# A graph layer on one core: one gather for the spare rows of two edge sets, and two sets given to the gathered path

## The chip, the cores and the metric

The kernel runs on one core of one Trainium2 chip. The metric is the device time of one execution in microseconds (us), taken as the median of several runs. TensorE is called PE in the profile (PEld is its weight loads), VectorE DVE, ScalarE ACT, GpSimd POOL; SP only issues DMAs here.

## The reference, cut to what matters

12,500 nodes with 128 features each, 400,000 edges, sorted by their destination. Each edge takes its source's row through one of two linear maps (by the edge's type), the results are summed by destination, a third map of the node itself is added, and relu, a residual and a layer norm follow:

```python
Xs = X[src]
m_data = Xs @ W_data.T + b_data
m_ctrl = Xs @ W_control.T + b_control
msg = jnp.where((edge_types == 0)[:, None], m_data, m_ctrl)
agg = jax.ops.segment_sum(msg, dst, num_segments=X.shape[0])
out = agg + (X @ W_self.T + b_self)
return jax.nn.relu(out)
...
x = _layernorm(x + _L0_gnn_ref(x, edge_index, edge_type_2, ...), axis=-1)
```

The kernel sums the raw source rows by destination and type first, and applies the maps to the sums.

## The kernel before, in words

**Rows.** Every row of x is split into three bf16 parts (384 values). They lie in SBUF as `x3`, in 98 blocks of 128 rows, and in device memory as `rows3`.

**Groups, chunks and sets.** The edges are 3125 chunks of 128. A group is 125 chunks, so there are 25 groups; each has five windows of 5 "p" chunks and 20 "e" chunks. `sets(g)` says how many of a group's five runs of 20 are handled as a *set*. In every fourth group it is all five, in the others four, and there the last window's 20 chunks go the way of the p chunks (25 in that window). This gives 107 sets and 985 gathered chunks. The main loop (L1066) has one turn, called a loop here, for each set `w`; `pairs` is the number of sets. Each loop takes its share of the gathered chunks, from the third loop on.

**The gathered path.** For a chunk, POOL issues one indirect DMA (`fetch`, L749 to L757) that brings 128 rows of 768 bytes from `rows3` into a tile `msg` (18 buffers), asked for 14 chunks ahead. `paced` (L759) ties each gather to a matmul on PE, so that it can't start before it; there are eleven such places in a loop, and a spare gather takes one of them before a chunk may. Later PE multiplies the rows by a 0/1 matrix of destinations, three matmuls and one for the counts (`gathered`, L772).

**The set path.** A set is 2560 edges. They are sorted into 100 cells, 98 of which stand for a block of 128 source rows, with 32 slots each. The cells lie as four quarters a (32 partitions each) by 25 columns q; column 24 holds blocks 96 and 97 and two empty quarters, 64 partitions. Two loops ahead of its use, the chain of set W runs (`give_slots`, L546): DVE builds the 0/1 matrix O of cells, PE counts the edges that stand ahead of each one (`before`, L579), DVE finds the ranks and the rank matrix, PE puts source row and destination code in their slots (`put`, L642), the slots are written to device memory and read back to all partitions (`spread`), DVE makes the pick matrix of them (L690), and the codes are turned and kept (`turn_codes` and `keep_codes`). In the set's own loop PE picks the rows out of `x3` by 98 matmuls (`pick`, L818), ACT copies them from PSUM (`rows`, L826), DVE makes the 0/1 matrix of destinations (`choose`) and PE adds (`add`, L847). This goes in five turns t = 0 to 4 (`unit`, L854); the end of a set (`end`, L883), with the last six columns, the chain's `tiled[5]` and the addition to the accumulator, is emitted within turn 0 of the next loop.

**Spare rows.** Edges with a rank of 32 or more find no slot. Up to 64 of them per set go to the spare half of column 24, and their rows come by a gather of 64 rows into the tile `last` (`spare_rows`, L796), issued in turn 1 of the set's loop and used by the last matmuls of the set. Its indices are made by `spare_slots` (L512) in four steps: a matmul that counts the spare edges of the partitions ahead (`over_before`, needs `over_n` of L619), a 0/1 matrix on DVE (`over_matrix`, tile `om_all`), seven matmuls (`turn`, needs `bits_b` of L629) and three copies on ACT (`keep`: the destination code, `part`, the index `idx`). For set w these steps ride in the chain of set w + 1: count and matrix after that chain's `before`, the last two in its `keep_codes`.

**PSUM.** All small products go through one bank, the tile `side` (one buffer): a chain's `ahead`, then its `rk`, the transposes of the finished groups and others take it in turn.

**Order.** Within an engine the instructions stand in an order that is planned when the program is built: mostly that of the code, but an instruction which the plan expects to wait may be passed by later ones. At run time each engine keeps its order. After every fourth or fifth loop a finished group is multiplied by the weights, normed and written (`finish`, L902), which makes those loops longer.

Of the kernel before, what the change touches and what calls it, by code (L numbers as in the profile page):

```python
# [17 lines left out]
P = 128  # L18
D = 128
# [10 lines left out]
NE = 5  # L30
# [10 lines left out]
CAP = 32  # L41
NBLK = -(-N // P)
NQ = 25
NCELL = 4 * NQ
OVF = 64
TOP = 7
# [104 lines left out]
def short_path(ctx, tc, const, ident, eps, wT, brow, bad, x, src, dst, etype, ws, bs, out):  # L151
# [23 lines left out]

    def sets(g):

        return NE if g % 4 == 0 else NE - 1

    def of_p(g, i):  # L180

# [111 lines left out]
    def iota(shape, pattern, base, mult, name):  # L293
        t = tmp.tile([P] + shape, I32, name=name)
        nc.gpsimd.iota(t, pattern=pattern, base=base, channel_multiplier=mult)
        return t
# [4 lines left out]
        nc.vector.tensor_copy(t, iota([n], [[1, n]], base, 0, f"{name}_i"))  # L301
        return t

    cell_col = keep.tile([P, NCELL], BF, name="cell_col")
    nc.vector.tensor_copy(cell_col.rearrange("p (a q) -> p a q", q=NQ), iota([4, NQ], [[1, 4], [4, NQ]], 0, 0, "i0"))
    for a, b in ((0, -1.0), (1, -1.0), (2, 96.0), (3, 97.0)):
        nc.vector.memset(cell_col[:, a * NQ + NQ - 1:a * NQ + NQ], b)
# [24 lines left out]
    slot_col = keep.tile([P, TOP, OVF], BF, name="slot_col")  # L332
    nc.vector.tensor_copy(slot_col, iota([TOP, OVF], [[-1, TOP], [1, OVF]], 0, 0, "i5"))

    om_all = keep.tile([P, TOP + 1, OVF], BF, name="om_all")
    nc.vector.memset(om_all, 0.0)

    ltri = keep.tile([P, 4, P], BF, name="ltri")
    free, own = iota([4, P], [[P // 4, 4], [1, P]], 0, 0, "i6"), iota([4], [[P // 4, 4]], 0, 1, "i7")
# [169 lines left out]
        )  # L509
        return sel  # L510

    def spare_slots(w, at):  # L512


        if w < 0:
            return [lambda: None] * 4
        s = slots[w]

        def over_before():
            nc.tensor.matmul(  # L520
                at["ahead"][:, 500:501], ltri[:, 0, :], over_n[:, w:w + 1], start=True, stop=True, skip_group_check=True
            )

        def over_matrix():
            s["om"] = om_all.rearrange("p k o -> p (k o)")
            nc.vector.tensor_scalar(om_all[:, :TOP], slot_col, at["ahead"][:, 500:501], None, op0=OP.is_equal)

        def turn():
            for k in range(TOP):
                nc.tensor.matmul(  # L530
                    at["rk"][:, 504:507], s["om"][:, k * OVF:k * OVF + P], s["bits"][:, :, k],
                    start=(k == 0), stop=(k == TOP - 1), skip_group_check=True,
                )

        def keep():
            code = s["code"][:OVF, NQ - 1:NQ]
            nc.scalar.copy(code, at["rk"][:OVF, 506:507].rearrange("p (n o) -> p n o", o=1).to_broadcast(list(code.shape)))
            part = two.tile([OVF, 2], FP, name="part")
            nc.scalar.copy(part, at["rk"][:OVF, 504:506])
            idx = two.tile([OVF, 1], I32, name="idx")  # L540
            nc.scalar.activation(idx, part[:, 0:1], AF.Identity, bias=part[:, 1:2], scale=128.0)
            s["idx"] = idx

        return [over_before, over_matrix, turn, keep]

    def give_slots(w):  # L546
# [32 lines left out]
        def before():  # L579
            s["ahead"] = side()  # L580
            cols = s["ahead"][:, :CQ * NCELL].rearrange("p (c j) -> p c j", j=NCELL)
            for a in range(4):
                cells = slice(a * NQ, (a + 1) * NQ)
                nc.tensor.matmul(  # L584
                    cols[:, :, cells], ltri[:, a, :], s["prod"][:, 2 * CQ:3 * CQ, cells],
                    start=(a == 0), stop=(a == 3), skip_group_check=True,
                )
            spares = s["spares"] = spare_slots(w - 1, s)
            spares[0]()

        def ranks():
# [80 lines left out]
        def keep_codes():  # L672
# [4 lines left out]
            nc.scalar.copy(code, at.to_broadcast(list(code.shape)))  # L677
# [116 lines left out]
        return evenly([lambda c=c: chunk(c) for c in range(n)])  # L794

    def spare_rows(w):  # L796
        msg = slots[w]["last"] = two.tile([P, 3 * D], BF, name="last")
        return nc.gpsimd.indirect_dma_start(  # L798
            out=msg[:OVF, :], out_offset=None, in_=rows3[:, :],
            in_offset=bass.IndirectOffsetOnAxis(ap=slots[w]["idx"], axis=0),  # L800
        )

    def picked(w, tiled, ending, before):

        g, i = each_e[w]
        s = {"sel": {}, "msg": {}}
        bounds = [0, 5, 10, 15, 19, NQ - 1]
        turns = len(bounds) - 1  # L810

        def choose(q0, n):

            sel = select(sp.tile([P, 10, 2 * EW], BF, name="esel")[:, :n], code_col, slots[w]["code"][:, q0:q0 + n])
            for k in range(n):
                s["sel"][q0 + k] = sel[:, k]

        def pick(ps, q, a0=0):  # L818
            for a in range(a0, 4):
                last = nc.tensor.matmul(  # L820
                    ps[CAP * a:CAP * (a + 1), :], slots[w]["pick"][:, a * NQ + q, :],
                    x3[:, 4 * q + a - a0].rearrange("p j d -> p (j d)"), start=True, stop=True, skip_group_check=True,
                )
            return last

        def rows(q, n, room, half=False):  # L826
            ps = psg.tile([P, room, 512], FP, name=f"got{room}")
            msg = two.tile([P, room, 3 * D], BF, name=f"emsg{room}")
            for k in range(n):
                last = pick(ps[:, k, :3 * D], q + k)  # L830
                s["msg"][q + k] = msg[:, k, :]
            if half:
                last = pick(ps[:, n, :3 * D], NQ - 1, 2)
            nc.scalar.copy(msg[:, :n], ps[:, :n, :3 * D])  # L834
            if half:
                nc.scalar.copy(s["msg"][NQ - 1][OVF:, :], ps[OVF:, n, :3 * D])
# [187 lines left out]

    def all_slots(w):
        units = begin_slots(w) + [u for _, u in begun.pop(w)]
        return units + [u for t in sorted(slots[w]["tiled"]) for u in slots[w]["tiled"][t]]

    split_units.pop(0)()
    prep_e(0)  # L1030
# [218 lines left out]
```

## Time and profile before

| | us |
|---|---|
| median of 3 runs (1748.27 to 1756.86) | 1756.15 |
| the profiled execution | 1757.87 |
| its span, first to last instruction | 1756.1 |

The profile is of one execution, whose granted TensorE clock was 0.995 of full speed on average. An engine's busy time is the time in which it executes; for PE the ends of matmuls are modelled. A row of a timeline has start, duration, engine, line, operation, the tiles written and read with their shapes, how many were merged into the row, and in brackets the engine's idle time before it with the instruction that ended it. A gather's duration on POOL is that of issuing it; the rows land later.

### The profile page before, as it was taken

To read this page: it belongs to the slowest core of one execution; us is meant where nothing else is said; L and a number is where in the kernel's file an instruction comes from. 1 tells how busy PE (TensorE), PEld (TensorE's weight loads), DVE (VectorE), ACT (ScalarE), POOL (GpSimd) and SP (SyncE) were. 2 spreads that over 40 slices of the span, in tenths; PEclk is the share of its full clock that TensorE was granted. 3 is DMA by queue.
4 is the path that set the end of the run, shared out by engine and by line. 5 is a ranking of instruction groups with operands and counts; after the bars stand their busy time and mean duration, and the time that the engine had idled before them with its cause. 6 is when DMAs were issued, how large, how long until landed. Compare 5 with 4: busy or idle time off the path is not lost.

```text
span 1756.1 us, 72083 instructions
## 1 busy us (share of the span) xinstructions
PE 1615.3 (92%) x29945; PEld 1311.7 (75%) x29945; DVE 1595.2 (91%) x3996; ACT 1229.2 (70%) x2249; POOL 1316.6 (75%) x1109
## 2 busy tenths in 40 slices
PE   0599999999999999999999999999999989999997
PEld 0377777777778777777877877777777777878786
DVE  8899999998999998999988999999999989999993
ACT  4577777767677667767766777776777766767675
POOL 0288877787777787877887877887877877777871
PEclk9999999999999999999999999999999999999999
DMA  8655454446454545444535454544454535544441
GB/s 237 209 165 160 128 158 136 147 125 199 115 164 134 159 125 179 143 152 127 166 119 164 150 164 133 164 122 147 160 159 135 158 108 162 167 139 141 151 139 41
DMA packets 190562, 261.28 MB, mean 149 GB/s; under 512 B 86437, under 2 KB 155983, under 8 KB 187152
## 3 DMA queue, kind: packets, MB, share of 16 engines
q1 hardware_dynamic: 126894, 148.02, 25.9%
q0 software_dynamic: 50704, 102.16, 20.8%
q10 hardware_dynamic: 12626, 6.40, 1.2%
q8 instruction: 236, 3.87, 0.9%
q14 instruction: 102, 0.84, 0.1%
HBM read 238.47 MB, written 18.00 MB: 146 GB/s over the span
## 4 chain that ended last, share of the span: by engine, by line
PE 48%; DVE 32%; issue 6%; DMA 6%; ACT 5%; DVEq 1%; POOL 1%; SPq 0%; POOLq 0%; ACTq 0%
PE sums L704 22%; PE got L820 15%; DVE esel L504 3%; PE side L950 3%; DVE pick L690 3%; PE sums L842 3%; DMA last<-rows,idx 3%; DVE rv L635 2%; ACT emsg L834 2%; DVE prod L598 2%; DVE prod L576 2%; PE side L584 2%; DVE acc L743 2%; PE side L647 2%; DVE ahead L594 2%
## 5 line engine op out<-in xcount | busy, mean ns | idle before, releaser
L754 POOL DMA_INDIRECT msg<-rows,pidx x985 | 1190.9, 1209 | 307.5 <-issue 118.9
L834 ACT CAST emsg<-got 128x768 bf16<-128x768 f32 (+1 forms) x1070 | 951.9, 930 | 303.9 <-PE got L820 289.8
L704 PE MATMUL sums<-esel,emsg 128*128 128x176 bf16 x7704 | 683.4, 240 | 0.0
L704 PEld LDWEIGHTS <-emsg 128*128 128x128 bf16 x7704 | 566.9, 98 | 68.7 <-issue 28.5
L820 PE MATMUL got<-x,pick 128*32 128x384 bf16 x10486 | 568.0, 330 | 21.9 <-DVE pick L690 14.7
L820 PEld LDWEIGHTS <-pick 128*32 128x32 bf16 x10486 | 239.2, 96 | 139.2 <-issue 20.6
L504 DVE TENSOR_TENSOR esel<-code_col,code 128x1760 bf16<-128x1760 bf16 x321 | 292.7, 912 | 13.6 <-PE sums L704 11.6
L798 POOL DMA_INDIRECT last<-rows,idx x107 | 122.0, 1141 | 106.0 <-DVE pick L690 63.7
L704 PE MATMUL sums<-psel,msg 128*128 128x48 bf16 x2955 | 184.2, 184 | 17.2 <-DVE acc L743 15.2
L842 PE MATMUL sums<-esel,one_col 128*32 128x176 bf16 x2675 | 193.7, 240 | 4.4 <-DVE acc L743 4.4
L704 PEld LDWEIGHTS <-msg 128*128 128x128 bf16 x2955 | 149.9, 97 | 36.2 <-issue 31.4
L842 PEld LDWEIGHTS <-one_col 128*32 128x32 bf16 x2675 | 111.9, 97 | 60.7 <-issue 4.1
L790 PE MATMUL sums<-psel,one_col 128*128 128x48 bf16 x985 | 150.2, 183 | 0.0
L743 DVE TENSOR_TENSOR acc<-acc,sums 128x352 f32 (+2 forms) x232 | 99.4, 430 | 40.4 <-PE sums L704 36.8
L504 DVE TENSOR_TENSOR O<-cell_col,blk 128x2000 bf16<-128x2000 bf16 x107 | 128.2, 1198 | 2.1 <-issue 2.1
L598 DVE TENSOR_TENSOR prod<-O,ahead 128x2000 bf16<-128x2000 bf16 x107 | 127.6, 1193 | 0.1
L690 DVE TENSOR_SCALAR pick<-pick,lane_f 128x3200 bf16<-128x3200 bf16 x107 | 113.2, 1058 | 0.0
L647 PE MATMUL side<-rv,O 128*128 128x64 bf16 x2140 | 83.3, 195 | 31.6 <-DVE rv L635 30.6
L647 PEld LDWEIGHTS <-O 128*128 128x128 bf16 x2140 | 78.7, 100 | 33.3 <-DVE rv L635 29.3
L594 DVE TENSOR_REDUCE ahead<-side 128x100 bf16<-128x500 f32 x107 | 72.2, 675 | 28.0 <-PE side L520 27.3
L790 PEld LDWEIGHTS <-one_col 128*128 128x128 bf16 x985 | 94.3, 96 | 0.0
L635 DVE TENSOR_TENSOR rv<-rm,vals 128x1280 bf16<-128x1280 bf16 x107 | 87.8, 821 | 0.3
(170 smaller groups left out, 1869.2 us busy)
## 6 DMA issues: line engine op xcount, KB each, us to landing
pick<-there SPq DMA_DIRECT2D x107, 800.0 KB
acc<-acc_start SPq DMA_DIRECT2D x23, 1280.0 KB
msg<-rows,pidx POOLq DMA_INDIRECT x985
rows<-x SPq DMA_DIRECT2D x6, 1344.0 KB
xs<-in_x_dram SPq DMA_DIRECT2D x99, 62.5 KB
out_dram<-h SPq DMA_DIRECT2D x99, 62.5 KB
xt<-in_x_dram ACTq DMA_DIRECT2D x6, 896.0 KB
there<-cell SPq DMA_DIRECT2D x107, 6.2 KB
```

The lines of the kernel that those rows point to most:

```text
L504: nc.vector.tensor_tensor(sel.rearrange("p n (w t) -> p n w t", t=2), col[:rows].rearrange("p (o w t) -> p o w t", o=1, t=2).to_broadcast( ...
L598: nc.vector.tensor_tensor(prod, s["O"], ahead.rearrange("p (o j) -> p o j", o=1).to_broadcast([P, EC, NCELL]), op=OP.mult)
L635: placed[:] = [nc.vector.tensor_tensor(rv.rearrange("p c v (r t) -> p c v r t", t=2), rm.rearrange("p c (o r t) -> p c o r t", o=1, t=2).t ...
L647: nc.tensor.matmul(s["rk"][:m, :2 * CAP], s["held"][:, c * NCELL:c * NCELL + m], s["rv"][:, c].rearrange("p v r -> p (v r)"), start=(c == ...
L690: nc.vector.tensor_scalar(t, t, lane_f, None, op0=OP.is_equal)
L704: last = nc.tensor.matmul(out, msg[:, j * D:(j + 1) * D], sel, start=(start and j == 0), stop=stop, skip_group_check=True)
L743: added.append(nc.vector.tensor_add(win, win, ps[:, :4 * wide].rearrange("p (a w) -> p a w", w=wide)[:, :, :width]))
L754: return nc.gpsimd.indirect_dma_start(out=msg, out_offset=None, in_=rows3[:, :], in_offset=bass.IndirectOffsetOnAxis(ap=codes["p", g][0][: ...
L790: nc.tensor.matmul(cnt, one_col, sel, start=False, stop=(c == n - 1), skip_group_check=True)
L820: last = nc.tensor.matmul(ps[CAP * a:CAP * (a + 1), :], slots[w]["pick"][:, a * NQ + q, :], x3[:, 4 * q + a - a0].rearrange("p j d -> p (j ...
L834: nc.scalar.copy(msg[:, :n], ps[:, :n, :3 * D])
L842: nc.tensor.matmul(cells_of(s["ps"], EW, 1)[CAP * (q % 4):CAP * (q % 4 + 1), :], one_col[:, :CAP], s["sel"][q], start=(q < 4), stop=(q + 4 ...
```

## The change

- `sets(g)` gives five sets in every sixth group instead of every fourth: 105 sets and 1025 gathered chunks.
- Even sets keep their layout: the spare rows in quarters 0 and 1 of column 24, blocks 96 and 97 in quarters 2 and 3. Odd sets are mirrored: blocks 96 and 97 lie in quarters 0 and 1, the spare rows in the other half. There are two tables of cells and two matrices `om_all`, one for each parity.
- One gather of 128 rows brings the spare rows of sets w and w + 1 (w even) into a tile `both` (one buffer). The odd set uses `both` directly. For the even set ACT copies the lower half into `last` (now one buffer) at the end of turn 4. The last set, 104, has no partner and is gathered alone, 64 rows.
- An odd set's spare slots are now made at the end of its own chain, so that both halves of the index are there for the even set's loop: `own_before` (count and matrix) goes with the code turns of the set's own chain and writes columns 508 and on of `rk`, `own_turn` (the seven matmuls and the three copies) comes at the end of turn 0 of the even set's loop. An even set's slots still ride in the next set's chain, which is odd; an even set's chain carries none.

```diff
     def sets(g):
-        return NE if g % 4 == 0 else NE - 1
+        return NE if g % 6 == 0 else NE - 1
...
-    om_all = keep.tile([P, TOP + 1, OVF], BF, name="om_all")
-    nc.vector.memset(om_all, 0.0)
+    om_all = [keep.tile([P, TOP + 1, OVF], BF, name=f"om_all{k}") for k in range(2)]
+    for t in om_all:
+        nc.vector.memset(t, 0.0)
...
-    def spare_slots(w, at):
+    def spare_slots(w, at, col=504):
...
-        def over_before():
+        def over_before(to="ahead", c=500):
+            s["before"] = at[to][:, c:c + 1]
             nc.tensor.matmul(
-                at["ahead"][:, 500:501], ltri[:, 0, :], over_n[:, w:w + 1], start=True, stop=True, skip_group_check=True
+                s["before"], ltri[:, 0, :], over_n[:, w:w + 1], start=True, stop=True, skip_group_check=True
             )
...
-            idx = two.tile([OVF, 1], I32, name="idx")
-            nc.scalar.activation(idx, part[:, 0:1], AF.Identity, bias=part[:, 1:2], scale=128.0)
-            s["idx"] = idx
+            part = two.tile([P, 2], FP, name="part")
+            nc.scalar.copy(part[half], at["rk"][half, col:col + 2])
+            if k == 0:
+                s["idx"] = two.tile([P, 1], I32, name="idx")
+            idx = slots[w - k]["idx"][half]
+            nc.scalar.activation(idx, part[half, 0:1], AF.Identity, bias=part[half, 1:2], scale=128.0)
...
-            select(s["O"], cell_col, blk2)
+            select(s["O"], cell_cols[w % 2], blk2)
...
-            spares = s["spares"] = spare_slots(w - 1, s)
+            spares = s["spares"] = spare_slots(w - 1 if w % 2 else -1, s)
...
+        def own_before():
+            s["own"] = spare_slots(w, s, 509)
+            s["own"][0]("rk", 508)
+            s["own"][1]()
+
+        def own_turn():
+            s["own"][2]()
+            s["own"][3]()
+
         s["tiled"] = {4: [put, spread], 5: [turn_codes, keep_codes]}
+        if w % 2:
+            s["tiled"][5] = [lambda: (turn_codes(), own_before()), keep_codes]
+            s["own_turn"] = own_turn
...
     def spare_rows(w):
-        msg = slots[w]["last"] = two.tile([P, 3 * D], BF, name="last")
+        n = P if w + 1 < pairs else OVF
+        both = two.tile([P, 3 * D], BF, name="both", bufs=1)
+        slots[w + 1 if n == P else w]["last"] = both
+        if n == P:
+            slots[w]["both"] = both
         return nc.gpsimd.indirect_dma_start(
-            out=msg[:OVF, :], out_offset=None, in_=rows3[:, :],
-            in_offset=bass.IndirectOffsetOnAxis(ap=slots[w]["idx"], axis=0),
+            out=both[:n, :], out_offset=None, in_=rows3[:, :],
+            in_offset=bass.IndirectOffsetOnAxis(ap=slots[w]["idx"][:n], axis=0),
         )
...
+        lead = 0 if w % 2 else 2
+        half_rows = slice(CAP * lead, CAP * lead + OVF)
...
             if half:
-                last = pick(ps[:, n, :3 * D], NQ - 1, 2)
+                last = pick(ps[:, n, :3 * D], NQ - 1, lead, lead + 2)
...
-                nc.scalar.copy(s["msg"][NQ - 1][OVF:, :], ps[OVF:, n, :3 * D])
+                nc.scalar.copy(s["msg"][NQ - 1][half_rows, :], ps[half_rows, n, :3 * D])
...
-            if t == 1 and w > 0:
+            if t == 1 and w > 0 and w % 2 == 0:
                 spare.append(lambda: spare_rows(w))
             if t == 3:
                 assert not spare
+                if "both" in slots[w]:
+                    slots[w]["last"] = two.tile([P, 3 * D], BF, name="last", bufs=1)
                 s["msg"][NQ - 1] = slots[w]["last"]
...
+            if t == 0 and w + 1 < pairs and "own_turn" in slots[w + 1] and w > 0:
+                slots[w + 1]["own_turn"]()
+            if t == turns - 1 and "both" in slots[w]:
+                nc.scalar.copy(slots[w]["last"][:OVF, :], slots[w]["both"][:OVF, :])
```

More of the change, by code (lines that the diff above doesn't have):

```diff
@@ L302, in table @@
         return t
[L304 to L307, printed above, removed]
+    cell_cols = [keep.tile([P, NCELL], BF, name=f"cell_col{k}") for k in range(2)]
+    cells_i = iota([4, NQ], [[1, 4], [4, NQ]], 0, 0, "i0")
+    for t, ends in zip(cell_cols, ((-1.0, -1.0, 96.0, 97.0), (96.0, 97.0, -1.0, -1.0))):
+        nc.vector.tensor_copy(t.rearrange("p (a q) -> p a q", q=NQ), cells_i)
+        for a, b in enumerate(ends):
+            nc.vector.memset(t[:, a * NQ + NQ - 1:a * NQ + NQ], b)
     rank_col = table(CAP, 0, "rank_col")
@@ L522, in over_before @@
             )
         def over_matrix():
-            s["om"] = om_all.rearrange("p k o -> p (k o)")
-            nc.vector.tensor_scalar(om_all[:, :TOP], slot_col, at["ahead"][:, 500:501], None, op0=OP.is_equal)
+            nc.vector.tensor_scalar(om[:, k:k + TOP], slot_col, s["before"], None, op0=OP.is_equal)
         def turn():
-            for k in range(TOP):
+            flat = om.rearrange("p k o -> p (k o)")
+            for j in range(TOP):
                 nc.tensor.matmul(
-                    at["rk"][:, 504:507], s["om"][:, k * OVF:k * OVF + P], s["bits"][:, :, k],
-                    start=(k == 0), stop=(k == TOP - 1), skip_group_check=True,
+                    at["rk"][:, col:col + 3], flat[:, j * OVF:j * OVF + P], s["bits"][:, :, j],
+                    start=(j == 0), stop=(j == TOP - 1), skip_group_check=True,
@@ L533, in turn @@
                 )
         def keep():
[L536 to L539, printed above, removed]
-            idx = two.tile([OVF, 1], I32, name="idx")
-            nc.scalar.activation(idx, part[:, 0:1], AF.Identity, bias=part[:, 1:2], scale=128.0)
-            s["idx"] = idx
+            code = s["code"][half, NQ - 1:NQ]
@@ new lines, in keep @@
+            nc.scalar.copy(
+                code, at["rk"][half, col + 2:col + 3].rearrange("p (n o) -> p n o", o=1).to_broadcast(list(code.shape))
+            )
+            part = two.tile([P, 2], FP, name="part")
[4 more added lines that the diff above has]
+            nc.scalar.activation(idx, part[half, 0:1], AF.Identity, bias=part[half, 1:2], scale=128.0)
@@ L816, in choose, with pick @@
                 s["sel"][q0 + k] = sel[:, k]
-        def pick(ps, q, a0=0):
-            for a in range(a0, 4):
+        lead = 0 if w % 2 else 2
+        half_rows = slice(CAP * lead, CAP * lead + OVF)
+        def pick(ps, q, a0=0, a1=4):
+            for a in range(a0, a1):
                 last = nc.tensor.matmul(
```

7 lines of the change are left out of this document (5 added, 2 removed).

## The prediction

> **What bounds the kernel now.** I read the page's first and fourth parts first, then the groups of instructions, the waits, and the stretches of the run. From the page:
>
> ```profile
> span 1756.1 us, 72083 instructions
> ...
> PE 1615.3 (92%) x29945; PEld 1311.7 (75%) x29945; DVE 1595.2 (91%) x3996; ACT 1229.2 (70%) x2249; POOL 1316.6 (75%) x1109
> ...
> PE 48%; DVE 32%; issue 6%; DMA 6%; ACT 5%; DVEq 1%; POOL 1%; SPq 0%; POOLq 0%; ACTq 0%
> ...
> L754 POOL DMA_INDIRECT msg<-rows,pidx x985 | 1190.9, 1209 | 307.5 <-issue 118.9
> ...
> L798 POOL DMA_INDIRECT last<-rows,idx x107 | 122.0, 1141 | 106.0 <-DVE pick L690 63.7
> ```
>
> By these shares POOL is idle for a quarter of the span, and the chain that ended last hardly touches it. The waits say otherwise (engine, line, releaser: us in total, times, longest):
>
> ```profile
> POOL msg L754 <- issue: 118.9, 390, 0.3
> POOL msg L754 <- PE got L820: 80.5, 249, 3.6
> POOL msg L754 <- PE sums L704: 51.9, 168, 1.0
> ...
> POOL last L798 <- ACT idx L541: 11.5, 5, 8.5
> ```
>
> 390 waits add up to 118.9 us and none is longer than 0.3: this is a fixed pause of 0.30 us after every gather, whoever is named as its releaser. The stretch in the middle shows what is left (PE, PEld, DVE, ACT and POOL busy):
>
> ```profile
> 82.00:1720.00 1638.00, 1570.09 (x29328) 1278.56 (x29325) 1515.15 (x3778) 1170.91 (x2166) 1301.01 (x1083) 1.00 0.48 147
> ```
>
> POOL works 1301.0 of 1638.0 us and pauses 1083 x 0.30 = 324.9, so only 12.1 us are free: **the gathers are a line without gaps**, 99% full. PE is 96% full, DVE 92%. PE does wait for POOL, at the spare rows, which have the shortest notice:
>
> ```profile
> PEld L704 <- DMA last<-rows,idx: 18.4, 14, 4.7
> PE sums L704 <- DMA last<-rows,idx: 15.2, 11, 4.5
> ```
>
> So POOL paces the kernel, and PE stands some 18 us behind it.
>
> **The change, part by part.**
>
> *Gathers.* Before, 985 chunk gathers and 107 spare gathers: 1092. After, 1025 chunk gathers and one spare gather for each pair, 53 (sets 0 and 1, ... , 102 and 103, then 104 alone): 1078, so 14 fewer. First and last start of either kind, with minimum, median and maximum ns:
>
> ```profile
> L754 POOL DMA_INDIRECT msg<-rows,pidx x985: 942/1043/4798, 73.2 to 1720.5; - x197
> ...
> L798 POOL DMA_INDIRECT last<-rows,idx x107: 911/1059/3007, 68.1 to 1729.9; - x107
> ```
>
> The start at 1720.5 is the 1091st (one spare gather follows): 1652.4 us over 1090 steps, 1.516 us each. 14 x 1.516 = **-21.2 us**. A pair's gather takes 128 rows where one took 64. The two kinds above are just these sizes: 942 ns against 911 at least, and the median of the larger is the smaller one. At most 52 x 0.031 = +1.6; I take **+1.6**, the lower end is 0.
>
> A gather is long where DVE works: one that starts beside a big DVE instruction takes 1.88 us, twice the minimum.
>
> ```profile
> 919.21 1.88 POOL L754 DMA_INDIRECT msg<-rows,pidx  x1 [0.30 <-DMA msg<-rows,pidx]
> ...
> 919.08 1.19 DVE L598 TENSOR_TENSOR prod<-O,ahead 128x2000 bf16<-128x2000 bf16 x1
> ```
>
> The time above the minima is 1190.9 + 122.0 - 985 x 0.942 - 107 x 0.911 = 287.5 us. Shared out over gathers it is in the 1.516. If it goes with the sets, whose DVE work the row shows beside a long gather, it is 2.69 us a set, and 14 x (0.942 + 0.30) + 2 x 2.69 = 22.8 us come off instead of 21.2. I keep 21.2 and 22.8 as the two ends. The Trainium skill ("SBUF — State Buffer", section "Who interferes with whom") says that a DVE instruction with two SBUF inputs contends with a GpSimd instruction that reads SBUF, which would make it the 22.8; the trace agrees as far as this row goes.
>
> *Two sets fewer, on PE.* A loop in which the chain of waits lies wholly on PE, between two ends of sets, and how closely chunks follow each other:
>
> ```profile
> 868.24 1.47 PE sums L704 x18
> ...
> 881.70 1.47 PE sums L704 x18
> ```
>
> ```profile
> 911.42 0.24 PE L704 MATMUL sums<-psel,msg 128*128 128x48 bf16 x3
> 911.50 0.18 PE L790 MATMUL sums<-psel,one_col 128*128 128x48 bf16 x1
> 911.53 0.23 PE L704 MATMUL sums<-psel,msg 128*128 128x48 bf16 x3
> ```
>
> 13.46 us a loop, 0.11 a chunk. With 985 / 105 = 9.4 chunks in it, a set alone costs 12.4: 2 x 12.4 - 40 x 0.11 = 20.5 us less on PE. Without the 18 us of stalls PE could end at 1756.1 - 18 - 20.5 = **1717.6**. PE therefore falls as much as POOL, and POOL stays ahead as the bound; none of PE's saving is added to the sum.
>
> *The odd set's own chain.* In every even loop, `own_before` (one matmul, 0.33 us on DVE) and `own_turn` (7 matmuls, three small ACT copies) stand beside the even set's; in odd loops the same work goes away, so the instruction count is nought. What is new are waits. The end of a set in the trace, by engine (PE, then ACT, DVE, POOL):
>
> ```profile
> 900.09 0.40 PE L704 MATMUL sums<-esel,last 128*128 128x176 bf16 x3 [3.04 <-DMA last<-rows,idx]
> 900.32 0.33 PE L530 MATMUL side<-bits_b,om_all 128*128 128x3 bf16 x7
> ...
> 902.17 0.41 PE L584 MATMUL side<-prod,ltri 128*128 128x125 bf16 x4
> ...
> 912.02 0.19 PE L667 MATMUL side<-ident_b,cell 128*32 128x25 bf16 x3
> 912.93 1.00 PE L820 MATMUL got<-x,pick 128*32 128x384 bf16 x20 [0.72 <-DVE pick L690]
> 913.76 0.18 PE L667 MATMUL side<-ident_b,cell 128*32 128x25 bf16 x1
> ...
> 915.02 0.39 PE L704 MATMUL sums<-esel,last 128*128 128x176 bf16 x3
> ```
>
> ```profile
> 900.84 0.16 ACT L539 COPY part<-side 64x2 f32<-64x2 f32 x1
> 901.03 0.29 ACT L541 ACTIVATE idx<-part 64x1 int32<-64x1 f32 x1
> 901.26 0.80 ACT L834 CAST emsg<-got 128x768 bf16<-128x768 f32 x1
> ...
> 908.52 0.47 ACT L836 CAST last<-got 64x384 bf16<-64x384 f32 x1
> ...
> 913.55 1.82 ACT L834 CAST emsg<-got 128x768 bf16<-128x768 f32 x2 [1.58 <-PE got L820]
> ```
>
> ```profile
> 903.22 0.33 DVE L526 TENSOR_SCALAR om_all<-slot_col,side 128x448 bf16<-128x448 bf16 x1
> ...
> 915.12 0.15 DVE L619 TENSOR_REDUCE over_n<-full 128x1 bf16<-128x8 f32 x1
> ...
> 911.83 1.15 POOL L798 DMA_INDIRECT last<-rows,idx  x1 [0.30 <-DMA msg<-rows,pidx]
> ```
>
> First wait: `own_before` follows the code turns (end 913.94) and needs that set's over_n, here at 915.27, so up to 1.3 us with the set's closing matmuls queued behind it on PE; nothing where over_n comes early. Second: `own_turn` writes the PSUM bank that ACT is reading until 901.00, so PE, done at 900.65, could stand 0.35 us. Third: the next chain's L584 takes the same bank; ACT would read the second turn only behind its 0.80 us copy, until about 902.4 instead of 901.0, and the copies of the next turns are behind that: 0.2 us late here. Lower end of all three together nothing, upper end 1.3 + 0.35 + 0.2 = 1.85 us in 52 loops, 96 us, on PE alone. I take 0.4 (over_n is late only in some loops), 21 us: that fits into the 24 us between PE's 1717.6 and the sum below, so **0** is added. POOL itself hardly waits: the indices stood ready at 901.32, the gather began at 911.83.
>
> The Trainium skill ("PSUM — Partial Sum Buffer", section "PSUM bank collisions raise a hardware error") says to guard PSUM with semaphores by bank and not by address, which speaks against putting a second set's columns into `rk`. The trace agrees that other columns of the bank are waited for:
>
> ```profile
> ACT code L677 <- PE side L530: 34.0, 58, 5.3
> ```
>
> (L677 reads columns 100 to 124, L530 writes 504 to 506.)
>
> *Landing.* The even set's rows go through `both` and are copied by ACT after its fourth turn. That copy (about the 0.47 of L836) has to be over when the copies of 913.55 begin, or these queue behind it: rows must land by 913.1 instead of 915.0, 1.9 us earlier, in 52 loops; the odd sets get a whole loop more. POOL may then run out of backlog somewhat oftener. Its free time is 12.1 us now; I take a third of that more, **+4**, with 0 and 12 as ends.
>
> *Start.* The first gather now waits for set 1's own chain too:
>
> ```profile
> 65.12 0.29 ACT L541 ACTIVATE idx<-part 64x1 int32<-64x1 f32 x1
> ...
> 68.07 2.96 POOL L798 DMA_INDIRECT last<-rows,idx  x1 [63.74 <-DVE pick L690]
> ```
>
> There are 2.7 us between index and gather. One more round (DVE 0.33, seven matmuls 0.33, ACT 0.16 + 0.29, with queues perhaps 3 us) is mostly covered; with the second tables on DVE I take **+1.5**, ends 0 and 3.
>
> Sum: -21.2 + 1.6 + 0 + 4 + 1.5 = -14.1 us. The profiled execution took 1757.87 us (span 1756.1); the median of the runs, 1756.15, is 1.7 below it. From the median: **1742 us**, 0.8% less.
>
> **The rivals.**
>
> *Slower: PE stalls at the odd set's chain.* If the three waits come to 1.2 us in each even loop, PE ends at 1717.6 + 52 x 1.2 = 1780. It decides above (1742 - 1717.6) / 52 = 0.47 us a loop, and is over the old time by 0.5% from (1765 - 1717.6) / 52 = 0.91. For it: PE is 96% full and runs its queue in order. Against it: the trace has PE taking later matmuls first (20 pick matmuls stand between the third and fourth code turn in the loop above).
>
> *No change: the earlier landing costs what the gathers save.* Half of PE's 14 stalls fall on even sets; each grows by 1.9 us (13), as many that were just missed cost 1 us (7), and the odd sets' 7 x 1.3 = 9 go away: 11 more, 1753.
>
> *The pairing saves POOL nothing, since 128 rows cost twice 64.* Then 52 x 1.14 = 59 us come on top, 1801. The rows of the two sizes stand against it.
>
> **How the numbers follow.** A measurement of this kernel tells about 0.5%, 8.8 us, from no change: faster is below 1747.4, slower above 1764.9. The forecast gets 0.60, its own range 1727 to 1747: all extra costs nought, the excess per set and half of POOL's free time gone give 1756.15 - 22.8 - 6 = 1727; the terms' upper ends, 1756.15 - 21.2 + 1.6 + 12 + 3 = 1751.6, run into the second rival. No change 0.15, PE's stalls 0.22, rows priced singly 0.03. Faster 0.60, same 0.15, slower 0.25. To hold 8 in 10 the range has to take in most of PE's stalls: 1727 to 1780.
>
> **What would show it.** Right: 1078 gathers, pauses of 0.30 us nearly throughout, about 1.51 us a step; spare gathers of 128 rows near 1.1 us; PE's waits for spare rows no longer than before. Wrong: POOL waiting for L541 or its gates by more than some 25 us in all; PE waits of over 0.5 us before the seven matmuls or L584 in every second loop; ACT waiting for a spare gather before the new copy.

## The result, and the profile after

| | us |
|---|---|
| before, median of 6 runs (1748.27 to 1760.87) | 1754.22 |
| after, median of 6 runs (1896.77 to 1904.9) | 1899.96 |
| after divided by before | 1.0833, 95% interval 1.0802 to 1.0863 |
| the profiled execution after, and its span | 1900.12, 1898.3 |

The change makes the kernel 8.3% slower; forecast was 0.8% faster, and the whole range is missed. The page of the kernel after, its first, fourth and fifth parts:

```profile
span 1898.3 us, 71594 instructions
...
PE 1650.1 (87%) x29637; PEld 1323.8 (70%) x29637; DVE 1583.7 (83%) x3948; ACT 1234.4 (65%) x2267; POOL 1286.2 (68%) x1095
...
PE 38%; DVE 22%; DMA 13%; issue 11%; ACT 7%; POOL 6%; SPq 1%; DVEq 1%; POOLq 0%; ACTq 0%
...
L774 POOL DMA_INDIRECT msg<-rows,pidx x1025 | 1219.6, 1190 | 476.1 <-PE sums L724 163.7
```

The work is about what was planned: 308 matmuls less on PE, 1025 + 53 gathers on POOL, DVE some 12 us less. Yet every engine has a smaller share of the span, and PE is *busier* with fewer matmuls (1650 us against 1615). No engine is as full as before, so the time went into waits. The kernel's list of waits names the place (engine, line, releaser: us in total, times, longest):

```profile
POOL msg L774 <- PE sums L724: 163.7, 243, 4.7
ACT last L914 <- DMA both<-rows,idx: 160.6, 50, 8.4
POOL msg L774 <- PE got L847: 144.9, 254, 3.9
...
DVE esel L507 <- PE sums L724: 120.6, 61, 8.5
...
PE got L847 <- ACT emsg L861: 94.9, 72, 6.9
```

L914 is the new copy from `both` to `last`. ACT waits there for the pair's gather in 50 of the 52 even loops, 3.2 us each time in the mean. The other rows are what follows: PE waits for ACT's copies of the picked rows, DVE for PE, and POOL, held by its gates, for PE. Before, these four rows (two of POOL, DVE, PE) had 51.9, 80.5, 11.6 and 5.8 us. A stretch of one even loop, rows of ACT, PE and POOL picked out:

```profile
973.79 0.79 ACT L861 CAST emsg<-got 128x768 bf16<-128x768 f32 x1
...
976.67 1.14 POOL L822 DMA_INDIRECT both<-rows,idx  x1 [0.30 <-issue]
...
979.96 0.51 ACT L914 COPY last<-both 64x384 bf16<-64x384 bf16 x1 [5.38 <-DMA both<-rows,idx]
980.37 1.80 ACT L861 CAST emsg<-got 128x1152 bf16<-128x1152 f32 x2
...
981.53 0.83 PE L847 MATMUL got<-x,pick 128*32 128x384 bf16 x8 [5.81 <-ACT emsg L861]
...
982.90 2.38 PE L724 MATMUL sums<-esel,emsg 128*128 128x176 bf16 x15
...
983.60 0.47 ACT L863 CAST last<-got 64x384 bf16<-64x384 f32 x1
...
986.47 1.86 ACT L861 CAST emsg<-got 128x768 bf16<-128x768 f32 x2 [2.40 <-PE got L847]
989.62 1.82 ACT L861 CAST emsg<-got 128x768 bf16<-128x768 f32 x2 [0.57 <-PE got L847]
```

ACT reaches the copy at 974.58, two microseconds before POOL even issues the gather, and stands there until 979.96. In the code the copy comes behind turn 4's two casts (here those of 986.47). The order planned at build time has put it ahead of them, of the three casts before them and of L863, right behind turn 2's first cast (that of 973.79). All those casts are queued behind a gather that has not been issued. In the other even loops it stands about as early: ahead of four to seven casts and L863, in 29 of the 52 loops ahead of six.

Two more things are to be read there. The fifteen matmuls of L724 take 2.38 us; the same fifteen took 1.31 in the kernel before (row further down). And the stretch's granted clock (columns: PE, PEld, DVE, ACT and POOL busy with instructions, clock, DMA share, GB/s):

```profile
970.00:975.50 5.50, 5.50 (x113) 4.50 (x110) 4.99 (x8) 4.15 (x7) 4.28 (x5) 1.00 0.64 228
975.50:981.50 6.00, 0.22 (x8) 0.00 (x0) 5.96 (x16) 1.54 (x3) 4.78 (x5) 0.87 0.28 66
981.50:986.50 5.00, 4.97 (x54) 3.66 (x57) 0.08 (x1) 1.98 (x4) 3.65 (x4) 0.50 0.26 71
986.50:991.50 5.00, 5.00 (x108) 4.50 (x100) 3.20 (x11) 4.43 (x9) 3.47 (x3) 0.98 0.25 65
```

After almost 6 us without matmuls PE works the next 5 us at half its clock: 54 matmuls where the following 5 us hold 108. So a long wait at the copy is paid twice, as idle time and as slow matmuls behind it.

### The profile page after: what moved, and what is told of

It reads as the page before. It is cut to its first block, busy times and chain, and to the rows that moved or that the text cites. A ratio compares the mean times of both kernels' runs of the same rounds, so it can differ in the third digit from the quotient of the medians.

```text
span 1898.3 us, 71594 instructions
## 1 busy us (share of the span) xinstructions
PE 1650.1 (87%) x29637; PEld 1323.8 (70%) x29637; DVE 1583.7 (83%) x3948; ACT 1234.4 (65%) x2267; POOL 1286.2 (68%) x1095
## 4 chain that ended last, share of the span: by engine, by line
PE 38%; DVE 22%; DMA 13%; issue 11%; ACT 7%; POOL 6%; SPq 1%; DVEq 1%; POOLq 0%; ACTq 0%
PE sums L724 17%; PE got L847 12%; DMA both<-rows,idx 8%; POOL msg L774 5%; ACT emsg L861 5%; PE side L983 3%; DVE esel L507 3%; PE sums L869 2%; DVE pick L710 2%; DVE prod L606 2%; PE side L655 2%; DVE rv L643 2%; DMA esrc<-in_src_dram 1%; DVE prod L584 1%; DVE ahead L602 1%
## 5 line engine op out<-in xcount | busy, mean ns | idle before, releaser
L774 POOL DMA_INDIRECT msg<-rows,pidx x1025 | 1219.6, 1190 | 476.1 <-PE sums L724 163.7
L861 ACT CAST emsg<-got 128x768 bf16<-128x768 f32 (+1 forms) x1050 | 935.0, 928 | 299.4 <-PE got L847 287.3
L724 PE MATMUL sums<-esel,emsg 128*128 128x176 bf16 x7560 | 692.9, 244 | 0.0
L847 PE MATMUL got<-x,pick 128*32 128x384 bf16 x10290 | 588.3, 335 | 114.8 <-ACT emsg L861 94.9
L724 PEld LDWEIGHTS <-emsg 128*128 128x128 bf16 x7560 | 575.3, 100 | 76.1 <-issue 49.6
L507 DVE TENSOR_TENSOR esel<-code_col,code 128x1760 bf16<-128x1760 bf16 (+2 forms) x315 | 287.7, 913 | 121.7 <-PE sums L724 120.6
L724 PE MATMUL sums<-psel,msg 128*128 128x48 bf16 x3075 | 190.0, 184 | 17.0 <-DVE acc L763 16.6
L724 PEld LDWEIGHTS <-msg 128*128 128x128 bf16 x3075 | 159.4, 98 | 34.4 <-issue 32.8
L822 POOL DMA_INDIRECT both<-rows,idx x53 | 62.9, 1187 | 109.9 <-DMA ptyp<-in_edge_type_dram 66.5
L914 ACT COPY last<-both 64x384 bf16<-64x384 bf16 x52 | 26.6, 512 | 160.8 <-DMA both<-rows,idx 160.6
L606 DVE TENSOR_TENSOR prod<-O,ahead 128x2000 bf16<-128x2000 bf16 x105 | 125.4, 1194 | 3.4 <-issue 1.1
L655 PE MATMUL side<-rv,O 128*128 128x64 bf16 (+1 forms) x2100 | 83.1, 196 | 33.7 <-DVE rv L643 33.4
L655 PEld LDWEIGHTS <-O 128*128 128x128 bf16 (+1 forms) x2100 | 79.0, 101 | 35.5 <-DVE rv L643 29.3
```

Source lines behind the costliest of these rows:

```text
L507: nc.vector.tensor_tensor(sel.rearrange("p n (w t) -> p n w t", t=2), col[:rows].rearrange("p (o w t) -> p o w t", o=1, t=2).to_broadcast( ...
L606: nc.vector.tensor_tensor(prod, s["O"], ahead.rearrange("p (o j) -> p o j", o=1).to_broadcast([P, EC, NCELL]), op=OP.mult)
L655: nc.tensor.matmul(s["rk"][:m, :2 * CAP], s["held"][:, c * NCELL:c * NCELL + m], s["rv"][:, c].rearrange("p v r -> p (v r)"), start=(c == ...
L724: last = nc.tensor.matmul(out, msg[:, j * D:(j + 1) * D], sel, start=(start and j == 0), stop=stop, skip_group_check=True)
L774: return nc.gpsimd.indirect_dma_start(out=msg, out_offset=None, in_=rows3[:, :], in_offset=bass.IndirectOffsetOnAxis(ap=codes["p", g][0][: ...
L847: last = nc.tensor.matmul(ps[CAP * a:CAP * (a + 1), :], slots[w]["pick"][:, a * NQ + q, :], x3[:, 4 * q + a - a0].rearrange("p j d -> p (j ...
```

## The experiments

Theory A of the first rounds: the place of the copy in ACT's queue is the loss. Rivals: the odd set's own chain stalls PE (the forecast's slower rival), and two sets fewer cost time by themselves. (In the rounds on the odd set's own turn, further down, Theory A is that this turn's place costs the rest.) In loop times, taken from the end of one set's last matmuls to the end of the next set's, even loops went from 15.7 to 18.8 us in the mean, odd ones from 15.5 to 15.7: the loss sits in the even loops, where the copy is, but also the own turn.

The runs were made on two kinds of chip. On one kind the kernel before takes 1752 to 1759 us (medians), on the other 2102 to 2104, and there the same edits come out differently; ratios are only set beside each other within one kind. A ratio is taken from the single runs, to the kernel before on the same chip, and can differ by up to 0.2% from the quotient of the medians. First come the runs on the kind of chip of the result.

### The copy's place

The edit ties the copy to stand behind turn 4's cast, where the code has it; nothing else is changed:

```diff
-            nc.scalar.copy(msg[:, :n], ps[:, :n, :3 * D])
+            s["cast"] = nc.scalar.copy(msg[:, :n], ps[:, :n, :3 * D])
...
-                nc.scalar.copy(slots[w]["last"][:OVF, :], slots[w]["both"][:OVF, :])
+                with tc.issue_after(s["cast"].ins):
+                    nc.scalar.copy(slots[w]["last"][:OVF, :], slots[w]["both"][:OVF, :])
```

> [...] Theory A (ACT blocked by the copy that stands too early): ACT's wait for both below 25 us, and a ratio to the kernel before of 0.985 to 1.005. Rival B or C (the pairing or the own chain itself is slow): 1.05 or more, as the changed kernel has.

The changed kernel itself was run beside it:

> The changed kernel as it is, for the same chip as the others: if this chip is like the first one, a ratio of 1.08 and some 160 us of ACT's wait for both. [...]

Measured: tied 1781.05 us, ratio 1.014 (1.011 to 1.017); as changed 1904.28, ratio 1.082 (1.0787 to 1.0853). **The place of one copy is worth 1904.28 - 1781.05 = 123 us.** The edit moves hardly anything else: in the two traces POOL's instructions run in the same order, ACT's differ in the 52 copies and a handful of others, and DVE's and PE's at a few places. Page and waits of the tied kernel, and an even loop of it:

```profile
span 1778.6 us, 71602 instructions
...
PE 1612.6 (91%) x29637; PEld 1298.0 (73%) x29637; DVE 1582.4 (89%) x3948; ACT 1232.6 (69%) x2267; POOL 1312.0 (74%) x1095
```

```profile
ACT last L915 <- DMA both<-rows,idx: 18.2, 11, 3.9
```

```profile
948.16 1.29 POOL L822 DMA_INDIRECT both<-rows,idx  x1 [0.30 <-issue]
...
951.62 0.47 ACT L863 CAST last<-got 64x384 bf16<-64x384 f32 x1
952.56 1.82 ACT L861 CAST emsg<-got 128x768 bf16<-128x768 f32 x2 [0.47 <-PE got L847]
954.41 0.51 ACT L915 COPY last<-both 64x384 bf16<-64x384 bf16 x1
```

The waits at the copy fall from 160.6 to 18.2 us, and the four rows that followed from them to 78.8, 83.3, 16.9 and 5.4. PE does the same 29637 matmuls in 1612.6 us instead of 1650.1: 37.5 of the 120 us of span were matmuls at a lower clock, the rest idle time. (In the two traces PE was busy at half its clock for 92.7 us and for 18.7; half of the difference is 37.) What is left over before is 1.4%, outside the 0.985 to 1.005 expected of Theory A: it does not explain all, and the forecast's -0.8% is not reached either.

### The number of sets

Two edits change only `sets(g)`: the tied kernel with the old 107 sets and 985 chunks (shown), and the kernel before with 105 sets and 1025 chunks (the reverse).

```diff
-        return NE if g % 6 == 0 else NE - 1
+        return NE if g % 4 == 0 else NE - 1
```

> The tied copy with the old 107 sets, 1039 gathers, again. If POOL paces the kernel before, freeing it of 53 gathers leaves PE's 1738 us plus new waits: a ratio of 0.99 to 1.00, above or below r1 by what the two sets are worth.

> The kernel before with 105 sets, 1130 gathers, again. The line of gathers paces: 58 us more, a ratio of 1.033. PE paces: 20 us less, 0.988. (On the chip of the first call, where POOL had free time, it was 1.0135.)

Measured: tied with 107 sets 1770.01, ratio 1.006 (1.0031 to 1.0089), above the 0.99 to 1.00 expected; before with 105 sets 1786.48, ratio 1.0176 (1.0143 to 1.0208), between the 1.033 and the 0.988 of the two theories. So the pairing by itself, with its copy mended, is not a gain but 0.6% of loss, and giving two sets away is a loss on its own: 28 us without the pairing, 1781.05 - 1770.01 = 11 with it. In the kernel before with 105 sets POOL and PE look like this over the middle stretch, the tied kernel with 107 sets beneath it:

```profile
82.00:1720.00 1638.00, 1533.64 (x28524) 1245.66 (x28527) 1477.89 (x3683) 1134.96 (x2096) 1296.89 (x1100) 0.99 0.49 146
```

```profile
82.00:1720.00 1638.00, 1573.51 (x29188) 1267.99 (x29185) 1515.50 (x3770) 1190.20 (x2209) 1243.78 (x1027) 1.00 0.49 146
```

With 105 sets and no pairing POOL is full: 1296.9 + 1100 x 0.30 = 1626.9 of 1638.0 us. As far as busy times tell, it paced that kernel, but its step is 1638 / 1100 = 1.489 us and not the 1.516 that the forecast took, and PE's waits for the spare rows rise with it:

```profile
PEld L704 <- DMA last<-rows,idx: 54.4, 27, 5.9
```

Before, that row had 18.4 us. With pairing and 107 sets POOL has 1638.0 - 1243.8 - 1027 x 0.30 = 86 us free: the gathers do not pace the kernel any more. PE, 96% full, is then the fullest; that it sets the pace is argued from the busy times.

The other side, the kernel before with 109 sets and 945 chunks (`g % 3`):

> The kernel before with 109 sets and 945 chunks. The prediction's prices: POOL -58 us, PE +20.5, floor 1756 - 18 + 20.5 = 1759, so 1.00 to 1.01, paced by PE. If a gather step is worth less than that (r3_before_105: 38 steps more cost 28 us, not 58), 107 is near the best split and 109 is 1.00 to 1.02. Under 0.995: POOL paced the kernel before and PE's price of a set was too high.

Measured: 1763.07 beside 1752.48, ratio 1.0054 (1.0033 to 1.0075). 107 is the best of the three splits for the kernel before, on this kind of chip. The forecast's prices would make two sets more 20.5 - 18 = 2.5 us slower; it was 10.6.

### The odd set's own turn

`own_turn`, seven matmuls and three copies, stood at the end of turn 0 of the even loop. The edit puts its matmuls directly behind the even set's seven in the odd set's `keep_codes`, and ACT's copies of both behind that:

```diff
         def keep_codes():
+            if w % 2:
+                s["own"][2]()
...
             s["spares"][3]()
+            if w % 2:
+                s["own"][3]()
...
-            if t == 0 and w + 1 < pairs and "own_turn" in slots[w + 1] and w > 0:
-                slots[w + 1]["own_turn"]()
```

> [...] On a chip on which the kernel before takes about 1757 us: Theory A (the wait between the two sevens and its place cost about 0.5 us in every even loop) 1750 to 1760, ratio 0.995 to 1.000, fast even loops at 13.6 us instead of 13.9. Theory B (the shift of the work to the even loops by itself): 1.004 to 1.010 as in r4_tied_107, fast even loops at 13.9.

> The same with 105 sets, the change as a whole with both places mended, against 1.014 in r1_copy_tied. Theory A: 1.003 to 1.008. Theory B: 1.012 to 1.016. It should be slower than s1_turns_107 by 10 us or so: then giving two sets away is a loss even with the pairing at its best; if it is faster, the two sets were right and only the two places were wrong.

Measured: with 107 sets 1761.33, ratio 1.0038 (1.0017 to 1.0059); with 105 sets 1764.95, ratio 1.0062 (1.0041 to 1.0084). With 105 sets that is Theory A: 1.014 to 1.0062, 14 us (10 us by the medians, each less its kernel before). With 107 sets Theory A's 0.995 to 1.000 is missed, and the step from 1.006 to 1.0038 lies within the intervals, so the times alone leave it open; the timelines show what became shorter. PE at the head of an even loop in the tied kernel with 107 sets:

```profile
994.02 0.33 PE L535 MATMUL side<-bits_b,om_all 128*128 128x3 bf16 x7
...
994.49 0.34 PE L847 MATMUL got<-x,pick 128*32 128x384 bf16 x1
994.76 0.34 PE L535 MATMUL side<-bits_b,om_all 128*128 128x3 bf16 x7
995.03 0.99 PE L847 MATMUL got<-x,pick 128*32 128x384 bf16 x19
...
996.03 0.41 PE L592 MATMUL side<-prod,ltri 128*128 128x125 bf16 x4
```

and with the own turn moved:

```profile
985.84 0.52 PE L535 MATMUL side<-bits_b,om_all 128*128 128x3 bf16 x14
...
986.51 1.00 PE L846 MATMUL got<-x,pick 128*32 128x384 bf16 x20
...
987.58 0.41 PE L592 MATMUL side<-prod,ltri 128*128 128x125 bf16 x4
```

From the first of the seven to L592 it is 2.01 us in the one and 1.74 in the other (medians of all even loops 2.01 and 1.73), and fast even loops of the two kernels are about 14.0 and 13.7 us long (13.46 before; 13.6 was expected). The profile gives the second seven's wait as a wait for ACT's reading of the bank only where it falls wholly into idle time, as here in the kernel as changed:

```profile
1011.58 0.33 PE L535 MATMUL side<-bits_b,om_all 128*128 128x3 bf16 x7 [0.57 <-ACT part L546]
```

Some 0.29 us in 51 even loops is 15 us, about what the 105-set pair of kernels shows. The edit moves the own turn and takes away the wait between the two sevens at once, and other small instructions shift with it; the runs do not part these. The waits for the rows at the copy were expected to fall and do not: with 105 sets 17.3 us in the kernel with the own turn moved (6 times, up to 4.4), 18.2 in the one without. With the chain mended and 107 sets a fast odd loop is 0.24 us shorter than before (13.22) and an even one 0.26 longer, so the two loops together take what they took.

The same with 109 sets:

> Copy tied, own turn in `keep_codes`, 109 sets and 945 chunks: 55 pair gathers, 1000 gathers in all. By the prediction's prices PE paces it, 20.5 us above s1_turns_107: ratio 1.007 to 1.013. If PE still waits for gathers with 107 sets, less than that. At most equal to s1_turns_107 if a set costs PE no more than 20 gathered chunks cost POOL.

Measured: 1787.17, ratio 1.0177 (1.013 to 1.0224), 26 us above the 107 sets: as expected in its direction, over the 1.007 to 1.013 in size, and a little over 20.5 us for two sets. With pairing, 109 is the worst of the three, and 105 and 107 are not told apart. None of the kernels tried on this chip beats the kernel before.

### The runs on the other chip

The first round of four has the edits above and one more: the copy emitted in `end()` and tied behind the first cast of the next loop's turn 0.

> The changed kernel with one edge more: the ACT copy of both into last may not be issued ahead of the ACT copy of the fourth turn's picked rows. Theory A (the copy stands too early in ACT's queue, ACT is blocked for 160.6 us, and PE and POOL behind it): ACT's wait for both falls below 25 us and the time to 1735 to 1765 us. Rival B (the gather for two sets comes too late wherever the copy stands): the wait moves with the copy, the time stays above 1850. Rival C (the waits of the odd set's own chain are the loss): 1850 or more, with PE or ACT waiting around L535, L546 and L592.

> The kernel before with 105 sets and 1025 gathered chunks, spare gathers as they were: 1025 + 105 = 1130 gathers, 38 more. The prediction's theory that the line of gathers paces the kernel: 38 x 1.516 = 58 us more, 1805 to 1815. The rival that PE paces and the gathers only look full: 20 us less, 1730 to 1740.

> As e1_copy_tied, but with the old 107 sets and 985 gathered chunks: 985 + 54 = 1039 gathers, 53 fewer than before. If POOL paces and the pairing works once the copy is tied, POOL is no longer the bound and PE's 1738 us (1756 less 18 us of stalls) plus new waits remain: 1740 to 1760. If e1 is faster than this, the two sets given away are worth their 40 gathers; if not, the pairing alone is the better kernel. Rival B or C: above 1850 here too.

> As e1_copy_tied, but the copy stands still later: behind ACT's copies of turn 0 of the next loop, just ahead of the set's last matmuls. Theory A: ACT hardly waits for both (under 8 us), but PE now waits for the copy itself, some 0.5 us in each even loop (26 us): between e1 and e1 + 30. If e1 still shows long waits for both (Rival B), this one is the faster of the two.

Measured, beside 2103.88 us for the kernel before: tied 2095.40, ratio 0.9965 (0.9936 to 0.9993); before with 105 sets 2132.08, 1.0135 (1.007 to 1.02); tied with 107 sets 2058.47, 0.9798 (0.9729 to 0.9867); copy later 2111.15, 1.0043 (1.0014 to 1.0071). A later place of the copy is thus no better than turn 4's: ACT does not wait for the rows in either kernel, and in the later one PE waits for the copy (6.0 us at its weight loads, 10 times).

> Copy tied behind turn 4's cast as in r4_tied_107, 107 sets and 985 chunks; the odd set's seven matmuls stand directly behind the even set's seven in `keep_codes`, and all their ACT copies come after both, so PE no longer waits between the two for ACT's reading of the bank. Theory A (what is left of the loss in r4_tied_107, 1770 beside 1759, is that wait and the place of own_turn at the head of the even loop): fast even loops fall from 14.0 to about 13.6 us, time 1750 to 1760, ratio 0.995 to 1.000. Theory B (the chain's other waits, or the shift of the work to the even loops itself): no change from r4_tied_107, ratio 1.004 to 1.010.

> The same with 105 sets and 1025 chunks, to be held against r1_copy_tied (ratio 1.014). Theory A: 10 to 20 us below it, ratio 1.003 to 1.008, and ACT's waits for the pair's rows at the copy fall below the 18 us of r1_copy_tied, since the indices are ready sooner. Theory B: ratio 1.012 to 1.016, and the same waits. Either way it stays above r5_turns_107 if giving two sets away costs time by itself (+28 us in the kernel before).

> The kernel before with 109 sets and 945 chunks, no other edit. The prediction's price of a gather step (1.516 us, 38 steps fewer, -58 us) would put POOL far below PE, whose floor by the prediction's 20.5 us for two sets is 1756 - 18 + 20.5 = 1759: ratio 1.00 to 1.01, paced by PE. If two sets fewer cost 28 us because PE's waits for late spare rows grow when POOL has more to issue, two sets more should cost less than 20 us: ratio 1.00 to 1.01 as well, with PE's waits for spare rows near nothing. If sets cost PE more than that, over 1.015. A ratio under 0.995 would say that 107 was not the best split of the kernel before.

Measured, beside 2102.44: own turn moved, 107 sets 2047.49, 0.9727 (0.9682 to 0.9773); the same with 105 sets 2072.82, 0.9855 (0.981 to 0.9901); before with 109 sets 2072.20, 0.9836 (0.9788 to 0.9884). Here the pairing is a gain, moving the own turn is one more with 105 sets (0.9965 to 0.9855; with 107 the intervals overlap), and without pairing 109 sets are faster than 107. A kernel that ran on both kinds of chip, the one before with 109 sets, tells the two apart. The chip of 2072 us first:

```profile
PEld L820 <- issue: 201.4, 394, 1.3
```

then the chip of 1763 us:

```profile
PEld L820 <- issue: 22.4, 65, 0.7
```

At these weight loads PE stands where nothing in the profile holds it, nine times as long. That is not the whole 320 us of span between the two: PE is idle for 303 us instead of 130, and its busy time, with the same 30253 matmuls, is 1778.8 us instead of 1631.7, at a mean granted clock of 0.970 instead of 0.996. The gathers, the casts and DVE's instructions last as long on the one as on the other (1194 and 1201 ns a gather, 929 and 930 ns a cast). Time and the count of gathers go together in three of these runs (38 more cost 28 us, 38 fewer save 30, the tied kernel's 53 fewer save 45), not in the mended kernel with 105 sets (14 fewer, 30 us saved). Why PE stands there stays open.

## Why the prediction was wrong, step by step

**The step that failed is "Landing".** It had the copy stand behind turn 4's casts, as the code has it, so that the rows would be due 1.9 us earlier, and priced that at +4 (0 to 12). The copy stood ahead of four to seven casts and L863 (five in the stretch shown), ACT reached it there before the gather was issued, and the wait was 160.6 us in all. Putting the copy where the step had assumed it takes 123 us off. The forecast had itself pointed to instructions that stand elsewhere than the code has them (the pick matmuls between two code turns), and took them as a help to PE; for the one new instruction that waits for a gather it did not ask which way the order could move. It also lacked the second half of the price: 37.5 us of slow matmuls after the stalls.

With the copy in its place the steps stand so:

- **Gathers, -21.2: wrong in size and in what it paces.** The price of 1.516 us a step is an average that holds the time lost beside DVE's work. In the kernel before with two sets fewer, 38 steps more cost 28 us, 0.74 a step. Its groups of gathers:

```profile
L754 POOL DMA_INDIRECT msg<-rows,pidx x1025 | 1210.8, 1181 | 318.5 <-issue 119.2
L798 POOL DMA_INDIRECT last<-rows,idx x105 | 121.6, 1158 | 102.0 <-DMA bias<-b_parts 63.8
```

40 chunk gathers more at the minimum and the pause, 40 x 1.242, less two spare ones, 2 x 1.211, are 47.3 us. But the time above the minima is 1210.8 + 121.6 - 1025 x 0.942 - 105 x 0.911 = 271 us (with the minima of before) where it was 287.5, 16 less, and 47.3 - 16 = 31 is about the 28 measured. The second end of the forecast, the excess by sets, was thus the nearer rule (47.3 - 2 x 2.69 = 42, where 38 x 1.516 = 58), though it gives too much as well; but it was weighed for 14 gathers together with two sets, where the two ends are 1.6 us apart, and not for the question that mattered: what giving two sets away costs POOL. With the pairing and 107 sets, 53 fewer steps brought nothing, which fits PE's pacing the kernel then; its distance, 18 us by the forecast's own reading of the stalls, was all there was to gain.
- **128 rows as 64: right.** All 53 spare gathers of the kernel after, and the 52 of pairs alone:

```profile
L822 POOL DMA_INDIRECT both<-rows,idx x53: 902/962/3298, 70.8 to 1872.0; - x53
...
L822 POOL DMA_INDIRECT both<-rows,idx x52: 941/976/3298, 70.8 to 1837.1; - x52
```

The 902 ns are the last gather's, of one set and 64 rows. The least for 128 rows is 941 ns against 911 for 64, the 0.03 us that the forecast allowed; the median is 976 against 1059.

- **Two sets fewer on PE, -20.5: the price of two sets more is near it** (26 us, paired and mended), but the saving was not to be had. In the mended kernels 105 sets take 1764.95 and 107 take 1761.33; the intervals overlap, so two sets fewer are not told from nothing there, and -21 is ruled out. The middle stretch of the mended kernel with 105 sets:

```profile
82.00:1720.00 1638.00, 1549.39 (x28927) 1257.12 (x28923) 1500.40 (x3725) 1173.20 (x2177) 1273.46 (x1064) 0.99 0.50 148
```

PE is 95% full and POOL, with its pauses of 1064 x 0.30 us, 97%: neither is a line without gaps.
- **The odd set's own chain, 0.4 us a loop on PE and 0 in the sum: the size was about right, the nought was not.** The second of its three waits, the bank, comes to about 0.29 us (0.35 was the bound). It was hidden in the sum by PE's distance of 24 us to POOL, and the kernels measured have no such distance: with 105 sets the own turn's place costs 10 to 14 us.
- **Start, +1.5 (0 to 3): too small.** In the kernel after the first spare gather starts at 70.8 (row above), 2.7 us later than before, at the upper end. Spare gathers of the kernel with 107 sets and both places mended:

```profile
L821 POOL DMA_INDIRECT both<-rows,idx x54: 897/946/3316, 71.9 to 1733.4; - x54
```

Before, they ran from 68.1 to 1729.9: the first is 3.8 us later and the last 3.5, and the span of the profiled execution is 3.6 longer (1759.7). What is left of the pairing's loss, 0.4%, is 3 to 10 us by its interval; that the later start is all of it is not shown.

Of the rivals, the slower one (PE stalls at the own chain) named a wait that is there, of a quarter of the size it needed. The no-change rival named the right transfer, the even set's rows due earlier, with 1.9 us where four to seven casts of ACT and L863 stood in between. The mechanism that decided was named only in the list of signs ("ACT waiting for a spare gather before the new copy"), with no price. Another sign came too, POOL waiting for its gates (163.7 and 144.9 us) and for the index (29.0); with the copy tied these are 78.8, 83.3 and 11.0.

By the medians, each less its kernel before, the 146 us part so: the copy's place 123, the own turn's place 10, two sets fewer 4 (not told from nothing), and the pairing with its later start 9. By the ratios the own turn's place is 14 and the pairing 7 (3 to 10), so only the first part is known well.

## What to carry to other kernels

Where the order within an engine is planned at build time, ask of every new instruction that waits for a DMA where the plan may put it, and what stands behind it: a half-microsecond copy in an in-order queue cost 123 us, and a tie to the cast it should follow got them back. An average price per instruction is not the price of one more or one less (1.516 us a gather in the mean, 0.74 for one more), and when two engines are both nearly full, relieving one of them is worth at most the distance to the other. Two small writes to one PSUM bank that another engine reads between them were better placed one directly behind the other (10 to 14 us here).

## What was not expected of the hardware

- PE's granted clock was 0.50 for about 5 us after 5.8 us without matmuls, and 0.98 after that. The Trainium skill ("TensorE: Matmul & The Clock Gate", "HAM oscillation — how this bites in real kernels") says that a wait longer than about 3.4 us lets the clock fall to half and the next burst starts cold; the rows above agree. In the kernel before, the fifteen matmuls that took 2.38 us there stand as

```profile
114.56 1.31 PE L704 MATMUL sums<-esel,emsg 128*128 128x176 bf16 x15
```

- Two kinds of chip run the same kernel in 1763 and 2072 us with nearly the same mean length of gathers, casts and matmuls (336 and 329 ns for L820); the difference is on PE, in part idle time that no wait of the profile explains. The mended pairing with 107 sets, which takes 53 gathers off POOL, was worth nothing on the one and 2 to 3% on the other.
- A gather of 128 rows is issued nearly as quickly as one of 64: 941 ns at least against 911.
